# A graph network on one core: two chains of work put between the pieces of the second convolution, in a written order

## The chip, the cores and the metric

The kernel runs on one core of a Trainium2 chip. The metric is the device time of one execution in microseconds, the median of several. A profile is one execution, recorded instruction by instruction; its span runs from the first instruction to the last. Engines: PE multiplies (PEld loads its weights), DVE does vector work, ACT activations, POOL (GpSimd) indirect loads, memsets and iotas; SP issues most DMAs.

## The reference, cut to what matters

Four layers work on a graph of 6250 nodes with 64 features and 206250 edges, sorted by destination, each self loop included; each layer adds its result to x after a layer norm and a ReLU.

```
h = relu(layernorm(x))
x = x + conv(relu(conv(h, W3, b3)), W4, b4)        # conv: D^-1/2 (A + I) D^-1/2 h W^T + b
x = x + segment_sum(norm * h[col], row)            # h = relu(layernorm(x)), over src
V = leaky(leaky(h) @ pAw + pAb) @ pBw + pBb        # h again from x
e = relu(relu(edge_attr @ w1 + b1) @ w2 + b2)
M = clip(sigmoid(e @ Bw + Bb) * V[src] + e @ Cw + Cb, 1e-5) ** 2
x = x + sqrt(segment_sum(M, dst) / count)
out = x + mean of h and three propagations of it   # h = relu(layernorm(x))
```

## The kernel before, in words

Nodes are padded to 49 blocks of 128; seven blocks make a chunk (CB = 7, W = 896 nodes, NC = 7). A is the matrix of edge counts, in fp8, kept in DRAM in seven chunks of columns A[c]; a piece (A[c], block rows k) is 128 x 6272 bytes, 784 KB. Node values are held as three bf16 parts (U3 and V3, written by `split`, L707), so a sum over three products stands for float32.

The stages, in order:

1. **Building A and the first convolution** (`fast`, L752 to L993). Fourteen strips of 448 columns are built on PE, ACT and DVE and written to DRAM by SP. Beside the build of one strip, `convolve` (L934) multiplies the strip before by U3 into p_sum. When a chunk's two strips are done, `hidden` (L947) turns its sums y to nodes (L739), adds the node's own value, normalises, turns it to features (L731), applies W3 with a ReLU (L960, L961) and W4 (L965), and splits the result into V3. `convolve` and `hidden` are generators; each `yield` is a place where the builder puts other work. The last chunk's `hidden(6)` has nothing after it: L991 runs it to its end behind the last `convolve`.
2. **The second convolution** (`gather`, L1001, first call L1047). For chunk c and row k, one piece is loaded (pool `apool`, 8 buffers) and multiplied by V3: 49 products of 128 x 192 into four banks p_acc (L1016), opened by a product of zeros (L1013). After the seventh piece DVE sums the three parts (L1024), and `convolved` (L1037) adds b4 and the residual, normalises, and splits into a new U3. The pools of this call are closed behind it.
3. **The gather over src** (second call of `gather`, from L1054), in pools opened anew. `turned` (L1056) does after each chunk the residual, the norm, the two node layers on PE (L1065, L1070, L1076, with ACT L1068 and L1072), adds pBb (L1079, L1081) and writes the chunk to Vp_dram by SP (L1082). Vp_dram is complete when the seventh is written.
4. **The messages' preparations** (L1096 to L1160): w1, w2, b1, b2, BC and the bias are loaded by ACT's queue, BC_b, src_g and dst_g (the edges' ends, `[128, 202, 8]` int32) by SP's; the bias is split in three (L1116 to L1120); `rel`, `off`, `missed` (L1139 to L1145) count edges that lie outside their window; `lane` (L1148, L1150) is dst modulo 128; `origin` (L1136) and `count` (L1157) are made by POOL.
5. **The messages** (L1161 to L1418): 202 groups of 1024 edges. A slot issues eight indirect loads (`fetched`, L1273 on: L1279 on POOL, from Vp_dram by src_g) into a pool of four v tiles, the edge layers (L1287 to L1305), the gate, the sum by destination, and the check that A is symmetric (`crossed`, `partial`). The order on PE, ACT and DVE is written out by hand there.
6. **Three propagations** (from L1420), the first from sums made beside the messages, two by `gather`.

Outside the hand-written stretch, a scheduler places each engine's instructions by its own estimate of when their inputs are ready; each engine and each DMA queue then works its list in order. A tile that takes up the memory of a closed pool waits for the last use of what lay there. [...]

Of the kernel before, what the change touches and what calls it, by code (L numbers as in the profile page):

```python
# [616 lines left out]
def fast(ctx, tc, bad, x, src, dst, edge_attr, W3, b3, W4, b4, w1, b1, w2, b2, Bw, Bb, Cw, Cb,  # L617
# [132 lines left out]

    X = node.tile([P, NB, D], F32, name="X")
    nc.scalar.dma_start(X, x.rearrange("(b p) f -> p b f", p=P))  # L752
    early = ExitStack()
    early_pool = early.enter_context(tc.tile_pool(name="early_pool", bufs=1, reuse_waits="tile"))
    with ExitStack() as ph:
# [52 lines left out]

        rpool = ph.enter_context(tc.tile_pool(name="rpool", bufs=3, reuse_waits="tile"))
        opool = ph.enter_context(tc.tile_pool(name="opool", bufs=2, reuse_waits="tile"))  # L810
        spool = ph.enter_context(tc.tile_pool(name="spool", bufs=3, reuse_waits="tile"))
        wpool = ph.enter_context(tc.tile_pool(name="wpool", bufs=1, reuse_waits="tile"))

        key = ipool.tile([P, 2, GC * P], BF16, name="key")
# [11 lines left out]
        with ExitStack() as ps:  # L826
# [109 lines left out]
            def convolve(s, strip):  # L936

                p = psum.tile([P, 512], F32, name="p_sum", bufs=2)
                for q in range(NQ):
                    for b in range(q * NB // NQ, (q + 1) * NB // NQ):  # L940
                        spread(p, U3, b, strip[:, b, :], CW)
                    yield
                if s % 2 == 0:
                    y[s // 2] = wpool.tile([P, W], F32, name="y")
                nc.scalar.activation(y[s // 2][:, s % 2 * CW:(s % 2 + 1) * CW], p[:, :CW], AF.Copy)

            def hidden(c):  # L947

                z = wpool.tile([P, CB, D], F32, name="z", bufs=2)
                nc.scalar.activation(z, to_nodes(psum, y[c], CB), AF.Copy)  # L950
                yield
                add_whole(z, U3, c)
                nc.vector.tensor_mul(z, z, over_features(norm0[:, blocks(c)]))
                yield
                zT = to_features(wpool, psum, z)
                yield
                h = wpool.tile([P, W], F32, name="h")
                for lo_, hi_ in ((0, 512), (512, W)):
                    p_h = psum.tile([P, 512], F32, name="p_node")
                    nc.tensor.matmul(p_h[:, :hi_ - lo_], W3T, zT[:, lo_:hi_], start=True, stop=True)  # L960
                    nc.scalar.activation(h[:, lo_:hi_], p_h[:, :hi_ - lo_], AF.Relu, bias=b3_c)  # L961
                    yield
                p_v = psum.tile([P, 512], F32, name="p_node").rearrange("p (b f) -> p b f", f=D)
                for k in range(CB):
                    nc.tensor.matmul(p_v[:, k, :], h[:, k * P:(k + 1) * P], W4T,  # L965
                                     start=True, stop=True)
                yield
                u = wpool.tile([P, CB, D], F32, name="z", bufs=2)
                nc.vector.tensor_mul(u, p_v[:, :CB, :], over_features(norm0[:, blocks(c)]))
                split(u, V3, c)  # L970

            beside = []
            for s in range(CS):
# [13 lines left out]
                nc.sync.dma_start(strip_of(s, slice(0, NB)), strip)  # L987
                beside = [convolve(s, strip)]
                if s and s % 2 == 0:
                    beside.append(hidden(s // 2 - 1))  # L990
            for steps in beside + [hidden(NC - 1)]:  # L991
                for _ in steps:
                    pass  # L993

# [3 lines left out]
        nc.vector.tensor_mul(u, h, over_features(scale[:, blocks(c)]))  # L998
        split(u, U3, c)

    def gather(apool, wpool, psum, U3, then):  # L1001


        zeros = wpool.tile([P, 6 * D], BF16, name="zeros", bufs=1)
# [1 line left out]
        for c in range(NC):  # L1006
            p = [psum.tile([P, 512], F32, name=f"p_acc{q}") for q in range(4)]
            for k in range(NC):
                t = apool.tile([P, CB, W], COUNT, name="piece")
                nc.sync.dma_start(t, A[c][:, blocks(k), :])  # L1010
                for d in range(CB):
# [3 lines left out]
                    for b in range(CB):  # L1015
                        nc.tensor.matmul(  # L1016
                            p[d // 2][:, d % 2 * 3 * D:(d % 2 + 1) * 3 * D],
                            t[:, b, d * P:(d + 1) * P],
                            U3[:, k * CB + b, :, :].rearrange("p t f -> p (t f)"),
                            start=False, stop=(k == NC - 1 and b == CB - 1 and d in (1, 3, 5, 6)))  # L1020
            z = wpool.tile([P, CB, D], F32, name="zg")
            for q in range(4):
                n = min(2, CB - 2 * q)
# [3 lines left out]
                    axis=AX.X, op=OP.add)  # L1027
            then(c, z)

    with ExitStack() as ph:
        wpool = ph.enter_context(tc.tile_pool(name="wpool", bufs=2, reuse_waits="tile"))
        U3 = of_nodes(node)
        with tc.tile_pool(name="apool", bufs=8, reuse_waits="tile") as apool, \
                tc.tile_pool(name="ps1", bufs=1, space=PSUM, reuse_waits="tile") as psum:

            def convolved(c, z):
# [2 lines left out]
                nc.vector.tensor_add(z, z, over_blocks(b4_r, CB))  # L1041
                nc.vector.tensor_add(X[:, blocks(c), :], X[:, blocks(c), :], z)
                h = wpool.tile([P, CB, D], F32, name="h")
                normed_and_split(h, U3, c, norm3)

            gather(apool, wpool, psum, V3, convolved)

        pAw_d = diagonal(pAw, "pAw_d", wpool)
        pBw_d = diagonal(pBw, "pBw_d", wpool)
# [43 lines left out]
    Y = part.tile([P, CS, CW], F32, name="Y")  # L1093
    piece_pool = ctx.enter_context(tc.tile_pool(name="piece_pool", bufs=3, reuse_waits="tile"))
    with ExitStack() as ph:
        cpool = ph.enter_context(tc.tile_pool(name="cpool", bufs=1, reuse_waits="tile"))  # L1096
        before = ExitStack()
        tpool = before.enter_context(tc.tile_pool(name="tpool", bufs=1, reuse_waits="tile"))
        w1_d = diagonal(w1, "w1_d")
        w2_d = diagonal(w2, "w2_d")  # L1100
        b1_c = column(b1, 2, "b1_c")
        b2_c = column(b2, 2, "b2_c")

        BC = cpool.tile([P, 4 * D], F32, name="BC")
        nc.vector.memset(BC, 0.0)
        for k in range(2):
            nc.scalar.dma_start(BC[k * D:(k + 1) * D, 2 * k * D:(2 * k + 1) * D], Bw)
            nc.scalar.dma_start(BC[k * D:(k + 1) * D, (2 * k + 1) * D:(2 * k + 2) * D], Cw)

        bias = tpool.tile([1, 4, 2, D], F32, name="bias")  # L1110
        for k in range(4):
            nc.scalar.dma_start(bias[:, k, 0, :], Bb.unsqueeze(0))
            nc.scalar.dma_start(bias[:, k, 1, :], Cb.unsqueeze(0))
        rest = tpool.tile([1, 4, 2, D], F32, name="rest")
        bias3 = [tpool.tile([1, 4, 2, D], BF16, name=f"bias{k}") for k in range(3)]
        nc.vector.tensor_copy(bias3[0], bias)  # L1116
        nc.vector.tensor_sub(rest, bias, bias3[0])
        nc.vector.tensor_copy(bias3[1], rest)
        nc.vector.tensor_sub(rest, rest, bias3[1])
        nc.vector.tensor_copy(bias3[2], rest)  # L1120
        BC_b = cpool.tile([3, 8 * D], BF16, name="BC_b")
        for k in range(3):
            nc.sync.dma_start(BC_b[k:k + 1, :], bias3[k].rearrange("o a b f -> o (a b f)"))
        ones = cpool.tile([3, P], BF16, name="ones")
        nc.vector.memset(ones, 1.0)

        src_g = cpool.tile([P, G, J], I32, name="src_g")
        nc.sync.dma_start(src_g, src.rearrange("(g p j) -> p g j", p=P, j=J))
        dst_g = tpool.tile([P, G, J], I32, name="dst_g")
        nc.sync.dma_start(dst_g, dst.rearrange("(g p j) -> p g j", p=P, j=J))  # L1130

        origin = tpool.tile([P, G], F32, name="origin")
        g0 = 0
        for g in range(1, G + 1):
            if g == G or window(g) != window(g0):
                nc.gpsimd.memset(origin[:, g0:g], float(window(g0) * QN))  # L1136
                g0 = g
        rel = tpool.tile([P, G, J], F32, name="rel")
        nc.vector.tensor_tensor(rel, dst_g, origin.unsqueeze(2).to_broadcast([P, G, J]),  # L1139
                                op=OP.subtract)  # L1140
        off = tpool.tile([P, G, J], F32, name="off")
        nc.vector.tensor_scalar(off, rel, float(P), None, op0=OP.is_ge)
        nc.vector.tensor_scalar(rel, rel, 0.0, None, op0=OP.is_lt)
        nc.vector.tensor_add(off, off, rel)
        nc.vector.tensor_reduce(missed[:, 1:2], off.rearrange("p g j -> p (g j)"), axis=AX.X,  # L1145
                                op=OP.add)

        nc.vector.tensor_scalar(dst_g, dst_g, P - 1, None, op0=OP.bitwise_and)  # L1148
        lane = cpool.tile([P, G, J], BF16, name="lane")
        nc.vector.tensor_copy(lane, dst_g)  # L1150
        own = cpool.tile([P, P // QN, 2], F32, name="own")
        nc.vector.memset(own[:, :, 0], 0.0)
        for q in range(P // QN):
            nc.vector.memset(own[q * QN:(q + 1) * QN, :q + 1, 0], 1.0)
        nc.vector.tensor_scalar(own[:, :, 1], own[:, :, 0], -1.0, 1.0, op0=OP.mult, op1=OP.add)
        count = cpool.tile([P, P, J], BF16, name="count")
        nc.gpsimd.iota(count, pattern=[[1, P], [0, J]], base=0, channel_multiplier=0,  # L1157
                       allow_small_or_imprecise_dtypes=True)

        before.close()  # L1160
        mpool = ph.enter_context(tc.tile_pool(name="mpool", bufs=3, reuse_waits="tile"))  # L1161
        ps_a = ph.enter_context(tc.tile_pool(name="ps_a", bufs=1, space=PSUM, reuse_waits="tile"))
        n1 = stat.tile([P, NB], F32, name="n1")
# [252 lines left out]
        nc.vector.tensor_add(of_all[:, 0:1], of_all[:, 0:1], of_all[:, 2:3])  # L1416
        nc.vector.tensor_copy(bad, of_all[0:1, 0:1])


    with ExitStack() as ph:  # L1420
        apool = ph.enter_context(tc.tile_pool(name="apool", bufs=6, reuse_waits="tile"))
# [85 lines left out]
```

## Time and profile before

| what | value |
|---|---|
| time, median of 3 runs | 4138.98 us (4115.52 to 4143.48) |
| the profiled execution: its time, its span | 3623.47 us, 3621.6 us |
| mean granted TensorE clock | 0.909 |
| busy: PE, DVE, ACT, POOL | 84%, 54%, 34%, 46% of the span |
| chain that ended last | POOL 35%, PE 34%, issue 15%, DMA 8%, DVE 7% |
| 570 to 586 us | PE 10.92, DVE 1.32, ACT 3.43 us busy, PEclk 0.71 |
| 586 to 790 us (second convolution) | PE 204.00, DVE 69.81, ACT 9.87, POOL 0.00 us busy |
| 1019 to 1057 us | PE 8.71, DVE 16.62, ACT 1.58, POOL 0.00 us busy, PEclk 0.61 |
| 1057 to 3137 us (messages) | PE 1672.00, DVE 1195.59, ACT 851.40, POOL 1586.87 us busy |

How to read it: the chain of work is followed back from the last instruction, at each step to what released it; a row of it is start, duration and what ran. A row of the timeline is start, duration, engine, line, operation, tiles, count, and in brackets how long the engine had been idle and what ended that. PEclk is the clock that the throttle granted to TensorE, as a share of full speed. The profile is of one execution; its time and the timed runs' differ by 515 us.

### The profile page before, as it was taken

The page shows a single profiled execution, that of the slowest core. Times are in us where ns is not written, and L with a number is a line of the kernel's source. Part 1 is how long each engine was busy: PE and PEld are TensorE (multiplying, and loading weights), DVE is VectorE, ACT ScalarE, POOL GpSimd, SP SyncE. Part 2 cuts the span into 40 slices and gives each one's busy share as a digit, 9 for nine tenths or more (in the row PEclk, how much of TensorE's full clock was granted, in tenths as well). Part 3 has the DMA queues.
Part 4 walks back from the last instruction along what each step waited for, and adds up shares of the span by engine and source line. Part 5 has one row for each costly group of instructions (what it writes and reads, how often), then busy time and mean ns, then how long its engine had stood idle before and what let it go on. Part 6 is the DMA issues. An engine that isn't in the chain of part 4 may idle for free.

```text
span 3621.6 us, 59158 instructions
## 1 busy us (share of the span) xinstructions
PE 3035.6 (84%) x24193; PEld 2135.5 (59%) x24193; DVE 1948.4 (54%) x3904; ACT 1243.4 (34%) x2031; POOL 1650.3 (46%) x1870
## 2 busy tenths in 40 slices
PE   1699999999967777778888788877888878799999
PEld 0466667999944444444444444444444444489999
DVE  6899993332235546555555655655655565531111
ACT  1577771000014334334444443433434443210000
POOL 4200000000027777777777777777777777400000
PEclk9999999999978888888889888888888888899999
DMA  3233335655582322323333333322332322256664
GB/s 107 62 91 95 95 95 193 197 180 178 174 103 70 86 54 66 88 70 94 78 80 89 78 78 81 92 70 70 97 88 70 93 70 76 80 162 196 196 207 143
DMA packets 280496, 388.75 MB, mean 107 GB/s; under 512 B 189226, under 2 KB 191332, under 8 KB 279956
## 3 DMA queue, kind: packets, MB, share of 16 engines
q1 hardware_dynamic: 222260, 323.17, 29.7%
q0 software_dynamic: 54112, 58.92, 8.6%
q8 instruction: 192, 3.15, 0.4%
q10 hardware_dynamic: 3840, 2.77, 0.3%
q14 instruction: 92, 0.75, 0.1%
HBM read 340.47 MB, written 44.24 MB: 106 GB/s over the span
## 4 chain that ended last, share of the span: by engine, by line
POOL 35%; PE 34%; issue 15%; DMA 8%; DVE 7%; ACT 1%; POOLq 0%; DVEq 0%; ACTq 0%
POOL v L1279 35%; PE p_acc L1016 21%; PE p_sum L748 6%; DMA v<-Vp_dram,src_g 5%; PE p_a L857 3%; DVE hd L848 1%; DVE lo L848 1%; PE p_node L739 1%; DMA near<-pairs,begin_i 1%; PE p_bc L1305 1%; DMA src_g<-in_src 0%; PE p_node L960 0%; DMA run<-pairs,exact_i 0%; PE p_acc L1013 0%; PE p_node L965 0%
## 5 line engine op out<-in xcount | busy, mean ns | idle before, releaser
L1279 POOL DMA_INDIRECT v<-Vp_dram,src_g x1616 | 1586.9, 982 | 541.0 <-issue 462.9
L1016 PE MATMUL p_acc<-U,piece 128*128 128x192 bf16 x9604 | 816.6, 247 | 3.9 <-DMA piece<-A 3.9
L1016 PEld LDWEIGHTS <-piece 128*128 128x128 fp8e4 x9604 | 799.2, 98 | 15.6 <-DMA piece<-A 4.4
L1305 PE MATMUL p_bc<-BC,h 128*128 128x256 f32 x1616 | 579.0, 491 | 0.0
L1314 DVE TENSOR_TENSOR m<-gate,v 128x512 f32<-128x512 f32 x202 | 140.0, 693 | 763.7 <-DMA v<-Vp_dram,src_g 332.4
L1305 PEld LDWEIGHTS p_bc<-BC,h 128*128 128x128 f32 x1616 | 338.7, 232 | 152.5 <-issue 114.6
L1321 ACT ACTIVATE m<-m 128x512 bf16<-128x512 f32 x202 | 127.2, 630 | 817.2 <-DVE m L1316 817.2
L1136 POOL MEMSET origin<- 128x1 f32 (+1 forms) x194 | 6.5, 97 | 859.1 <-DMA piece<-A 859.1
L1024 DVE TENSOR_REDUCE zg<-p_acc 128x128 f32<-128x384 f32 x112 | 56.8, 508 | 598.7 <-PE p_acc L1016 598.2
L748 PEld LDWEIGHTS <-U 128*64 128x64 bf16 x4116 | 230.3, 113 | 217.4 <-issue 72.1
L861 ACT ACTIVATE strip<-p_a 128x784 fp8e4<-128x784 f32 x392 | 301.8, 820 | 104.0 <-PE p_a L857 103.0
L1301 PE MATMUL p_bc<-BC_b,ones 3*128 3x512 bf16 x404 | 179.2, 443 | 159.9 <-DVE m L1315 159.9
L1188 PE MATMUL p_sum<-ident_b,piece 128*128 128x128 bf16 x1372 | 154.1, 237 | 180.2 <-DVE junk L1194 179.9
L1188 PEld LDWEIGHTS <-piece 128*128 128x128 fp8e4 x1372 | 117.0, 106 | 314.8 <-issue 297.3
L1301 PEld LDWEIGHTS <-ones 3*128 3x128 bf16 x404 | 37.4, 93 | 431.4 <-DVE m L1315 231.2
L1291 PE MATMUL p<-h,w_d 128*128 128x512 f32 x404 | 255.7, 719 | 40.8 <-ACT h L1295 40.8
L748 PE MATMUL p_sum<-piece,U 128*64 128x448 fp8e4 x2058 | 238.4, 374 | 28.9 <-DVE junk L1194 20.7
L1295 ACT ACTIVATE h<-p,b_c 128x512 f32<-128x512 f32 x404 | 255.9, 684 | 13.5 <-PE p L1291 13.5
L1194 DVE SCALAR_TENSOR_TENSOR junk<-p_sum,there 128x512 bf16<-128x512 f32 (+1 forms) x392 | 242.4, 618 | 19.6 <-DMA there<-A 6.0
L748 PE MATMUL p_sum<-strip,U 128*64 128x448 fp8e4 x2058 | 236.8, 359 | 2.9 <-ACT U L711 1.4
L848 DVE TENSOR_TENSOR lo<-count,key 128x2048 bf16<-128x2048 bf16 x196 | 238.3, 1216 | 0.0
L857 PEld LDWEIGHTS <-lo 128*128 128x128 bf16 x3136 | 164.9, 103 | 102.7 <-DVE lo L848 80.3
(186 smaller groups left out, 3478.1 us busy)
## 6 DMA issues: line engine op xcount, KB each, us to landing
piece<-A SPq DMA_DIRECT2D x249, 784.0 KB
e<-in_edge_attr SPq DMA_DIRECT2D x202, 256.0 KB
A<-strip SPq DMA_DIRECT2D x14, 2744.0 KB
v<-Vp_dram,src_g POOLq DMA_INDIRECT x1616
there<-A SPq DMA_DIRECT2D x28, 784.0 KB
pairs<-pair SPq DMA_DIRECT2D x1, 1616.0 KB
Vp_dram<-v SPq DMA_DIRECT2D x7, 224.0 KB
out<-X SPq DMA_DIRECT2D x6, 224.0 KB
```

The lines of the kernel that those rows point to most:

```text
L748: nc.tensor.matmul(p[half * D:(half + 1) * D, :w], U3[:, b, k, :], at_block, start=(i < 2), stop=(i >= 3 * n - 2))
L848: nc.vector.tensor_tensor(t, of.unsqueeze(1).to_broadcast(t.shape), key[:, k, at:at + GB].rearrange("p (h j) -> p h j", j=GQ) .unsqueeze(2 ...
L857: nc.tensor.matmul(p[:, j, :2 * NB], lo[:, g // GQ, :, g % GQ], hd[:, g // GQ, :, g % GQ], start=True, stop=True)
L861: nc.scalar.activation(strips[s][:, :, col:col + 2 * SG].rearrange("p b (j l) -> p b j l", l=2), p[:, :, :2 * NB].rearrange("p j (b l) -> ...
L1016: nc.tensor.matmul(p[d // 2][:, d % 2 * 3 * D:(d % 2 + 1) * 3 * D], t[:, b, d * P:(d + 1) * P], U3[:, k * CB + b, :, :].rearrange("p t f - ...
L1188: nc.tensor.matmul(p[:, a - a0, :], held["here"][:, a, b * P:(b + 1) * P], ident_b, start=True, stop=True)
L1194: nc.vector.scalar_tensor_tensor(junk[:, :(a1 - a0) * P], p[:, :a1 - a0, :].rearrange("p a q -> p (a q)"), 15.5, there, op0=OP.min, op1=OP ...
L1279: nc.gpsimd.indirect_dma_start(out=v[:, j, :], out_offset=None, in_=Vp_dram[:, :], in_offset=bass.IndirectOffsetOnAxis(ap=src_g[:, g, j:j ...
L1291: nc.tensor.matmul(of[g][p], w, of[g].pop(x), start=True, stop=True)
L1295: nc.scalar.activation(of[g][t], of[g].pop(p), **how)
L1301: nc.tensor.matmul(p_bc[:, 4 * b:4 * b + 4].rearrange("p j o f -> p (j o f)"), ones, BC_b, start=True, stop=False)
L1305: nc.tensor.matmul(p_bc[:, 2 * q:2 * q + 2].rearrange("p j o f -> p (j o f)"), h2[:, q * P:(q + 1) * P], BC, start=False, stop=(k == 1))
```

## The change

- `hidden(NC - 1)` is no longer run behind the first convolution. It is given the second convolution's pools and its steps are issued between that one's pieces.
- The preparations of stage 4 become a generator, `prepared`, whose steps follow those of `hidden` in the same places. Its results lie in a pool at the other end of the memory (`side="right"`), where the strips' pool is moved too, and stay until the messages end.
- `gather` takes the steps (`beside`): two after each of the first five pieces of chunk 0, then one after each piece. The first call runs under a hand-written order for PE and DVE.
- BC, the bias and BC_b are loaded by GpSimd. src and dst are no longer loaded in runs of eight ints: four loads by GpSimd bring rows of 1024 ints (`rows_i`, 101 partitions), DVE turns them to float32, PE transposes them 4 x 101 columns at a time into a bank p_turn (two banks), and DVE copies them into src_g and dst_g.
- The second convolution's `apool` has 7 buffers for 8. The new U3 is made at the first chunk's end. The y of the last two strips lies in the pool that V3 lies in.

```diff
-        spool = ph.enter_context(tc.tile_pool(name="spool", bufs=3, reuse_waits="tile"))
+        spool = ph.enter_context(tc.tile_pool(name="spool", bufs=3, side="right", reuse_waits="tile"))
...
-                    y[s // 2] = wpool.tile([P, W], F32, name="y")
+                    y[s // 2] = (wpool if s < CS - 2 else early_pool).tile([P, W], F32, name="y")
...
-            for steps in beside + [hidden(NC - 1)]:
+            for steps in beside:
...
-    def gather(apool, wpool, psum, U3, then):
+    def gather(apool, wpool, psum, U3, then, beside=iter(())):
...
+                for _ in range(2 - (c > 0 or k > 4)):
+                    next(beside, None)
...
+    def prepared(psum):
+
+        cpool = apart.enter_context(tc.tile_pool(name="cpool", bufs=1, side="right", reuse_waits="tile"))
...
+            nc.gpsimd.dma_start(BC[k * D:(k + 1) * D, 2 * k * D:(2 * k + 1) * D], Bw)
...
+        def row(i):
+            rows_i.append(tpool.tile([GH, P, J], I32, name="rows_i", bufs=2))
+            nc.gpsimd.dma_start(rows_i[i], halves_of[i][0])
+
+        row(0)
+        row(1)
+        for _ in range(6):
+            yield
+        for i in range(4):
+            rows_f = tpool.tile([GH, J, P], F32, name="rows_f", bufs=2)
+            nc.vector.tensor_copy(rows_f, rows_i[i].rearrange("g p j -> g j p"))
+            if i < 2:
+                row(i + 2)
+            yield
+            for j0 in range(0, J, 4):
+                p = psum.tile([P, 4, GH], F32, name="p_turn", bufs=2)
+                for j in range(4):
+                    nc.tensor.transpose(p[:, j, :], rows_f[:, j0 + j, :], ident[:GH, :GH])
+                nc.vector.tensor_copy(halves_of[i][1][:, :, j0:j0 + 4],
+                                      p.rearrange("p j g -> p g j"))
+                yield
...
-        with tc.tile_pool(name="apool", bufs=8, reuse_waits="tile") as apool, \
+        with tc.tile_pool(name="apool", bufs=7, reuse_waits="tile") as apool, \
...
-            gather(apool, wpool, psum, V3, convolved)
+            with tc.manual_schedule(engines={ET.PE, ET.DVE}):
+                gather(apool, wpool, psum, V3, convolved, (
+                    step for steps in (hidden(NC - 1, wpool, psum), prepared(psum))
+                    for step in steps))
...
-        src_g = cpool.tile([P, G, J], I32, name="src_g")
-        nc.sync.dma_start(src_g, src.rearrange("(g p j) -> p g j", p=P, j=J))
-        dst_g = tpool.tile([P, G, J], I32, name="dst_g")
-        nc.sync.dma_start(dst_g, dst.rearrange("(g p j) -> p g j", p=P, j=J))
...
+        cpool, w1_d, w2_d, b1_c, b2_c, BC, BC_b, ones, src_g, lane, own, count = made.pop()
```

The lines left out of `prepared` are those of stage 4, cut in steps by `yield`: the bias and BC_b, then `rel`, then `off` and `missed`, then `lane`, `own` and `count`.

## The prediction

> **What bounds the kernel now.** I read the slices of the page first (PE at 0.9 in the first third, then POOL at 0.7 while PE stays at 0.7 to 0.8), then the chain that ended last, then the timeline around the change. The chain gives PE 34% and POOL 35% (all L1279) of the span: first PE bound, then, from 1057 to 3137 us, bound by GpSimd's 1616 fetches. Two places in between are bound by neither. The chain in order of time, at the end of the first convolution:
>
> ```profile
> 556.74 14.16 PE p_sum L748 x147
> 570.90 1.75 PE p_node L739 x14
> 577.48 2.08 PE p_node L960 x2
> 580.33 1.66 PE p_node L960 x2
> 582.64 3.25 PE p_node L965 x14
> 586.21 2.24 PE p_acc L1016 x14
> 588.77 1.93 PE p_acc L1016 x14
> 592.18 24.83 PE p_acc L1016 x301
> ...
> 790.73 4.57 DMA piece<-A
> ```
>
> Between 570.90 and the first p_acc work at 585.68 stands one chain through PE, ACT and DVE (`hidden(6)`), with nothing beside it. The p_acc groups of 14 after it take 2.24 us and 1.93 us, where 301 take 24.83 us (82.5 ns each, so 14 take 1.16). At 790.73 the gather by src waits 4.57 us for its first piece.
>
> The same view, from the end of that gather to the first fetch:
>
> ```profile
> 1000.64 17.83 PE p_acc L1016 x216
> 1018.48 0.02 issue
> 1018.49 17.71 DMA src_g<-in_src
> ...
> 1037.19 5.25 DMA bias<-in_L_gnn_Cb
> ...
> 1043.00 7.77 DMA BC_b<-bias
> 1050.77 1.83 DVE rel L1139
> ```
>
> 38.6 us pass between the last matmul on this chain and the first fetch, and they go to loading and preparing, in series. The timeline shows who waits for whom:
>
> ```profile
> 1036.80 0.30 ACT L701 ACTIVATE v<-v,eps 128x7 f32<-128x7 f32 x1 [38.09 <-DMA bias<-in_L_gnn_Bb]
> 1053.23 0.39 SPq L1082 DMA_DIRECT2D Vp_dram<-v  x1
> 1057.11 2.33 POOL L1279 DMA_INDIRECT v<-Vp_dram,src_g  x1 [48.75 <-DVE lane L1150]
> ```
>
> The last chunk's own work (its ACT square root) is held at 1036.80 behind the bias loads on ACT's queue, its addition of pBb behind `rel` on DVE, and the fetch waits for `lane`.
>
> **What the Trainium skill says.** "TensorE: Matmul & The Clock Gate", section "What's actually happening": an idle window of some 3.4 us halves the array's clock, and about as much work restores it. The trace agrees: PEclk is 0.79 at 576 to 577, 0.50 from 577 to 590, 0.88 in the next us. "DMA: Bandwidth & Descriptors", section "Why small descriptors are slow": each packet carries a fixed cost. The trace agrees: src_g, 808 KB in runs of 8 ints (32 B), took 17.71 us while the DMA share stood at 1.4 to 2.0 and 54 to 69 GB/s moved, where pieces move at 400 to 450 GB/s (568 to 584 us). Section "Issuing engines are not separate DMA queues": loads from GpSimd share the 16 engines, so the row loads will run among the pieces; no run shows that yet.
>
> **The change part by part**, against the profiled span of 3621.6 us. A minus is time gained.
>
> *Start.* The built order shows W3's and W4's loads now behind five square roots on ACT's queue, and the copy to W3T ahead of the 25 L802 counts on DVE. The fifth root ran at 32.48. The load then takes 2.65 us (as the small `near` gathers do) to 4.5 us (10.58 to 15.04 before), with PE 0.76 us: ready at 36.0 to 37.8, where DVE got there at 36.0. I take +1.0 (0 to +2.5).
>
> *hidden(6) into the gather.* Before: p_acc would have had to start at 587.92 to be, at full pace, where it was at 590.54 (two groups of 1.31 us back), so the stretch costs 587.92 - 570.90 = 17.0. After: pieces flow from 568.5 at about 0.4 MB/us, so the first lands near 571 and PE waits about 1.3. hidden's PE work at full clock is 1.71 (14 by 122 ns) + 0.60 + 0.45 + 1.12 (as L1070 in the gather) + 0.84 + 1.71 = 6.4. Its steps are issued in pairs, so PE still sits through the feature copies (1.0 and 0.57) and the last ReLU (0.67): 2.2; 0.6 for changing over. 17.0 - 10.5 = **-6.5** (-4 to -8.5). The other waits (y, z) pass under a piece of 4.1 us. V3's last block is ready after piece 3 and read at piece 6.
>
> *Pieces' pool, 8 to 7.* The 49 pieces end in slot 6, not 0. In the built program the next gather's first five pieces wait for matmuls of the last chunk's pieces 0 to 4, not for its last one. Before: 790.71 to 795.35 idle, then 112 matmuls in 10.90 us (9.24 at full pace): 6.3. After: the four zero matmuls wait for the last sum, ended at 791.09: 0.8. **-5.5** (-4 to -6). Seven buffers are still 28 us ahead.
>
> *Preparations into the gather, on PE.* 32 transposes of 101 columns; four of 128 took 0.66 (L1065), so 8 x 0.52 = 4.2. DVE is in written order: chunk 0's chain ends 10.9 us after chunk 1's first matmul (627.76 - 616.85), the first row cast comes behind it, and its transposes behind piece 1, at 8.75. The cast of 1024 ints in strides takes 0.63 (by L1150's 0.99 for 1616) to 1.17 (by L1139's 1.84); I take 1.1: PE waits 12.0 - 8.7 = 3.3. Later transposes find their cast done and their bank read (17 against 12). **+7.6** (+4.5, no stall, to +15, one us for each group).
>
> *The same on DVE, ACT, POOL.* About 21 us of DVE (four casts, eight copies of some 0.55, bias 2.6, the L1139 to L1150 group 9.5) lie in a stage where DVE worked 70 of 204 us; chunk ends stay clear: chunk 2's `rel` ends near 28, its first sum is wanted at 27 and PE needs it by 30. Were that cover gone, `rel`'s 1.8 would be added. POOL is idle there; its memsets and iota stand ahead of the waits. Behind the later row loads only BC_b waits on POOL. ACT's four diagonal loads wait for early pieces and stand before chunk 0's square root, 15 us ahead of need. The rows (404 KB each) cost, by the page's 2.0 + bytes/436e3 us ("Anatomy of one DMA"), an estimated 2.9 us. The third row is asked for at 12 and wanted near 31, so 0.
>
> *After the gather.* Gone from the path: src_g, dst_g, eight bias loads, BC_b, rel and lane. What remains is the chunk's chain. In chunk 5 it went from L1057 at 990.01 to the write's issue at 1001.40: 11.4. The last one runs at half clock (1.09, 2.08, 2.04 against 0.66, 1.12, 1.16): +2.3. From 1022.93 it issues at 1036.6. Then the write must land: at most 3.6 (1053.23 to 1056.84); by the page's formula about 2.5. I take 3.0 and 0.3: fetch at 1039.9. 1057.1 - 1039.9 = **-17.2** (-15.5 to -18.5).
>
> Does the earlier start reach the end? POOL's fetches idle 541 us, 462.9 of it their own issue, 48.8 this start, 25.6 buffers. So it is passed on in full. The first e load follows the write at once; PE starts on it some 5 us after the fetch, as before.
>
> Sum: 1.0 - 6.5 - 5.5 + 7.6 - 17.2 = -20.6: span 3601. The profiled execution took 3623.5, the timed runs 4139 (4115.5 to 4143.5); no view shows the 515 us between, so I subtract the same time: **4118**.
>
> **Rivals.**
> - *The earlier fetches are not passed on*: the messages end with something else, and the first three parts alone are left (-3.4): 4136. For it: PE is busy 80% there. Against: the chain stays on L1279. 0.09.
> - *Timed runs stretch the removed waits*: they are 14% longer than the profile. If the removed loads and waits are what is stretched, about double, the gain is 41: 4097 or less. Against: 14% as such makes 23.5. 0.12.
> - *Row loads late*: DVE stands at the third cast (chunk 1, piece 6), the chunk's sums are queued behind it, PE waits for them. Each us beyond 31 adds one. Slower than before from 19 of margin + 20.6 of gain, a load of 40 us; at 60 it gives 4139 + 20 = 4159. For it: 14 pieces queue on the same engines. Against: src_g, twice the bytes in small packets, took 17.7. 0.06.
> - *The moves do not happen* is excluded: the built order shows them on PE, DVE, POOL and SP.
>
> **How the numbers follow.** The forecast has 0.73, its own range 4103 to 4133 (the parts' ends, and the three runs' scatter of 28). About 1%, 41 us, is what a measurement of this kernel can tell from no change. Faster by more: 0.13 (the second rival and an edge of scatter). Slower by more: 0.04, of the third. Within: 0.83. The range that leaves out 2 in 10 is 4092 to 4143.
>
> **What would show it.** p_acc starts near 572 with groups of 14 near 1.2 us from the start; p_node and p_turn between pieces; one PE wait for the first cast of about 3 us; no wait for a piece at the next gather; the fetch some 17 us after the last sum, released by the Vp_dram write. Wrong if PE waits for rows or DVE at chunk ends, if the gather of the first stage grows by over 25 us, or if the fetches' stretch (2080 us) grows.

## The result, and the profile after

| | before | after |
|---|---|---|
| median of 20 runs | 4141.14 us | 4125.14 us |
| lowest to highest | 4115.52 to 4176.94 | 4093.77 to 4160.34 |
| ratio, 95% interval | | 0.9954 (0.9935 to 0.9973) |

The ratio is 19 us in 4141 (11 to 27); it leaves out the runs that count as slow, over 1.5% above the fastest of their kernel, while the two medians, 16 us apart, are those of all 20 runs. The forecast was 4118 us, the kernel before less 20.6. The profiled execution of the kernel after has a span of 4132.5 us and a clock of 0.847.

The times of one and the same kernel come in two sets, by the group of runs. In one the medians of the kernel before are 4141 to 4171 us, and single runs lie up to some 40 us to either side; in the other it takes 3619 to 3627 us. Each group of the experiments ran on one chip, so the text speaks of chips of the first kind (the long times) and of the second; that it is the chip, and not something else about the group, is not shown. The first profile of the kernel before (3621.6 us) is of the second kind, the profile of the kernel after is of the first. So stages are compared here from the moment when SP issues the last strip's write, and the kernel before was profiled again on a chip of the first kind (`before_again`, below). Those two profiles give, in us after the strip's write ("in between" is the change since the row above):

| | before_again | after | difference | forecast |
|---|---|---|---|---|
| strip's write issued (from the start) | 562.29 | 562.66 | +0.4 | +1.0 |
| chunk 1 of the second convolution starts | 59.96 | 56.73 | -3.2 | -6.5 |
| last chunk ended, next gather opens | 233.64 | 238.86 | +8.5 in between | +7.6 |
| chunk 1 of the src gather starts | 267.85 | 267.93 | -5.1 in between | -5.5 |
| last sum on DVE ended | 465.60 | 465.66 | 0.0 in between | 0 |
| first fetch | 499.84 | 482.70 | -17.2 in between | -17.2 |

The first fetch comes 17.1 us sooner. Where that comes from can be read in the views of the kernel after. Its chain of waits at the end of the first convolution:

```profile
563.28 17.35 DMA piece<-A
580.67 1.37 PE p_acc L1017 x14
582.36 2.24 PE p_acc L1017 x14
584.92 1.38 PE p_acc L1017 x14
586.46 0.58 PE p_acc L1017 x7
587.03 1.54 PE p_node L739 x14
588.57 4.04 PE p_acc L1017 x49
...
603.38 15.61 PE p_acc L1017 x189
```

`hidden(6)` now stands between pieces (p_node after seven products of p_acc), as the change says. But the first piece lands 17.35 us after its issue. p_sum is done at 576.9 (ACT copies y at 576.88), so PE waits 3.8 us for the piece, where 1.3 was forecast, and the second group of 14 takes 2.24 us, where 1.16 is the full pace: half clock again.

The preparations take time from PE in chunk 1 (first the timeline, then the chain):

```profile
630.94 1.07 DVE L1073 CAST rows_f<-rows_i 101x1024 f32<-101x1024 int32 x1
632.07 0.56 PE L1080 MATMUL p_turn<-ident,rows_f 101*128 101x101 f32 x4 [3.78 <-DVE rows_f L1073]
```

```profile
632.63 5.70 PE p_acc L1017 x49
638.33 0.35 PE p_turn L1080 x4
638.68 8.09 PE p_acc L1017 x98
```

PE waits once, 3.78 us, for the first cast. Then a piece of 49 products takes 5.70 us, where two pieces take 8.09 (4.04 each). After the first one, a group of four transposes takes 0.35 us; 0.52 was forecast.

At the next gather there is no wait for a piece, only the one for the last sum:

```profile
801.69 0.77 PE p_acc L1014 x4
802.46 27.56 PE p_acc L1017 x334
```

And the end of the src gather, in the chain and in the timeline:

```profile
1033.83 1.10 PE p_node L1175 x4
1035.02 0.61 ACT hT L1178
1035.66 2.09 PE p_a L1180 x2
1037.78 0.70 ACT aT L1182
1038.49 0.70 DVE aT L1183
1039.33 2.06 PE p_v L1186 x8
1042.13 2.20 DMA Vp_dram<-v
```

```profile
1045.36 1.03 POOL L1325 DMA_INDIRECT v<-Vp_dram,src_g  x1 [363.51 <-issue]
```

src_g, the bias, `rel` and `lane` are gone from this stretch. What is left is the last chunk's own work on PE, about twice as long as in the other chunks (2.09 and 2.06 us where p_a and p_v take 1.14 and 1.16), and its write.

### The profile page after: what moved, and what is told of

It is laid out like the page before. It is cut to its first block, busy times and chain, and to the rows that moved or that the text cites. A ratio compares the mean times of both kernels' runs of the same rounds, so it can differ in the third digit from the quotient of the medians.

```text
span 4132.5 us, 59248 instructions
## 1 busy us (share of the span) xinstructions
PE 3161.0 (76%) x24225; PEld 2164.1 (52%) x24225; DVE 1984.4 (48%) x3916; ACT 1257.3 (30%) x2031; POOL 1663.9 (40%) x1889
## 4 chain that ended last, share of the span: by engine, by line
PE 51%; DVE 16%; another core or an unknown queue 13%; issue 9%; ACT 7%; DMA 2%; POOL 1%; DVEq 0%; SPq 0%; ACTq 0%; POOLq 0%
PE p_acc L1017 18%; PE p_sum L748 9%; PE p_bc L1351 7%; PE p L1337 5%; PE p_a L858 3%; DVE junk L1240 2%; ACT h L1341 2%; PE p_s L1379 2%; DVE m L1361 2%; DVE m L1360 2%; PE p_bc L1347 2%; PE p_e L1333 2%; DVE m L1362 1%; ACT gate L1356 1%
## 5 line engine op out<-in xcount | busy, mean ns | idle before, releaser
L748 PE MATMUL p_sum<-piece,U 128*64 128x448 fp8e4 x2058 | 272.4, 384 | 80.9 <-issue 59.6
L1337 PE MATMUL p<-h,w_d 128*128 128x512 f32 x404 | 270.0, 752 | 73.6 <-ACT h L1341 58.8
L1424 ACT ACTIVATE m<-m 128x512 bf16<-128x512 f32 x202 | 127.3, 630 | 594.0 <-DVE m L1423 468.6
L1379 PE MATMUL p_s<-m,to 128*128 128x192 bf16 x1616 | 207.0, 276 | 117.9 <-DVE r_s L1387 61.7
L1337 PE MATMUL p<-eT,w_d 128*128 128x512 f32 x404 | 250.2, 705 | 17.7 <-issue 8.1
L1367 ACT ACTIVATE m<-m 128x512 bf16<-128x512 f32 x202 | 127.2, 630 | 431.0 <-DVE m L1362 342.8
L1379 PEld LDWEIGHTS <-to 128*128 128x128 bf16 x1616 | 174.1, 150 | 145.3 <-issue 141.3
```

The source lines that it names most:

```text
L748: nc.tensor.matmul(p[half * D:(half + 1) * D, :w], U3[:, b, k, :], at_block, start=(i < 2), stop=(i >= 3 * n - 2))
L1337: nc.tensor.matmul(of[g][p], w, of[g].pop(x), start=True, stop=True)
L1379: nc.tensor.matmul(p, to[:, :, j], m3[:, j].rearrange("p t f -> p (t f)"), start=(j == 0), stop=(j == J - 1))
```

## The experiments

**The kernel before again (`before_again`, no edit).**

> The kernel before, unchanged, profiled again beside the others. Question: where do the 515 us lie that the timed runs of before take over its first profile (3621.6), and do the stretches that the change removes get longer with them? Theory (the forecast's): they lie elsewhere, in the messages above all (the kernel after spends some 2500 us there, against 2080 in the first profile of before), and from the last sum of the src gather to the first fetch it stays near 38.6 us, from the first convolution's strip to the end of chunk 0 near 60.3 us. Rival (removed waits are stretched): those two stretches are some 14% to 100% longer, 44 to 77 us and 69 us up, and the change should have brought more than it did. Span expected near 4137 by both.

The span is 4169.4 us. From the last sum to the first fetch it takes 34.2 us, as in the first profile (466.19 to 500.39 after the strip's write), and from the strip's write to chunk 1 it takes 59.96 us against 60.13. So the stretches that the change removes are not longer on this kind of chip, and the rival of stretched waits falls. (The expectation's 38.6 counts from PE's last product, not from the sum.) The time lies in the fetches: from the first to the last it is 2604.7 us against 2078.1, 526.6 more. Another 5.6 lie before the strip's write, and 16 behind the last fetch. In the fetches the chain that ended last is another one. Its shares by engine over the whole of before_again:

```profile
PE 53%; DVE 16%; another core or an unknown queue 12%; issue 9%; ACT 7%; DMA 2%; POOL 1%; DVEq 0%; SPq 0%; POOLq 0%; ACTq 0%
```

In the first profile POOL had 35% of it; here it has 1%. GpSimd waits 550.6 us, in 106 waits, for DVE (L1314) to give back a v tile, and DVE, ACT and PE in turn stand still for stretches whose releaser no view names.

**One part alone: `hidden(6)` (`hid_only`).** From the kernel before: the strips' pool, the y of the last two strips and the new U3 as in the kernel after, and

```
-            gather(apool, wpool, psum, V3, convolved)
+            with tc.manual_schedule(engines={ET.PE, ET.DVE}):
+                gather(apool, wpool, psum, V3, convolved, hidden(NC - 1, wpool, psum))
```

> One part alone: only hidden(6) goes between the pieces; the preparations stay behind the src gather and are loaded as before, and the pieces' pool keeps its eight buffers. In the profile of the kernel after, the stretch from the strip's write to the end of chunk 0 shrank by 3.9 us, not by the forecast 6.5: the first piece came 17.4 us after its issue and PE idled 3.8 us for it. Theory A: the eight bias loads and the two row loads that GpSimd issues at the same moment took engine time ahead of that piece. Then here, without them, the first p_acc comes some 15 us after the strip's write is issued, PE idles under 2 us, no clock is lost, and the stretch is 53.5 to 55 us against 60.3 (gain 5.5 to 7). Theory B: the piece would have come no sooner anyway; then p_acc comes 18 us after and the gain is 3.9 again. The median: 4 to 7 us below the kernel before (ratio 0.998 to 0.999), within what the rounds can tell.

The first product into p_acc comes 15.5 us after the strip's write (the piece is issued at 564.34 and takes 14.83), so PE waits the forecast 1.3 us. Every group of 14 takes 1.16 to 1.33 us, and chunk 1 starts at 52.55, 7.4 us sooner than before. Theory A holds: without GpSimd's loads the part is worth its forecast, and a little more. With eight buffers the next gather's chunk 0 takes 34.34 us. The first fetch comes at 494.39, only 5.4 sooner: here SP's queue has src_g behind the last Vp_dram write, and the fetch waits for that load (17.12 us). The ratio is 0.9955 (0.9924 to 0.9986). The interval just leaves out what 5.4 us would give (0.9987), and no view explains why the timed runs gain more than the earlier fetch.

**The other part alone: the preparations (`prep_only`).** From the kernel after:

```
-            for steps in beside:
+            for steps in beside + [hidden(NC - 1, wpool, psum)]:
...
-                gather(apool, wpool, psum, V3, convolved, (
-                    step for steps in (hidden(NC - 1, wpool, psum), prepared(psum))
-                    for step in steps))
+                gather(apool, wpool, psum, V3, convolved, prepared(psum))
```

> The other part alone: hidden(6) runs to its end behind the first convolution as before, only the preparations go between the pieces (two steps after each of the first five), with seven buffers. Theory: fetch 17 us after the last sum (38.6 before, so about -21 with the cold chain's start counted alike), no wait for a piece at the next gather (-5.5), PE longer by 8 transposes groups and one wait for the first cast. The steps come eight earlier than in the kernel after, so the first cast stands in chunk 0, before any chunk's chain holds DVE: PE's wait for it should be about 1 us or none, not 3.8, and the gather of this stage +3 to +4 us rather than +8.4. Sum -19 to -22: ratio 0.9945 to 0.9955, so nearly all of the gain of the whole change. Rival (the earlier fetches are not passed on): ratio 0.999 to 1.0.

The end of the src gather is as expected (17.0 us from the last sum to the first fetch), and that gather's chunk 0 takes 29.07. PE's part is not as expected. There is no wait for a cast in chunk 0, but the third row's cast falls behind chunk 0's chain on DVE, and PE waits for it 4.34 us in chunk 1, which takes 36.57. That is the same wait at another cast. The first fetch comes at 486.29, 13.5 us sooner. The ratio is 0.9981 (0.9956 to 1.0007), that is 8 us less, with an interval from 18 less to 3 more: it holds the 13.5 and does not tell it from nothing.

**Is an earlier fetch passed on? (`late_fetch`)** The kernel after, with

```
+                if c == NC - 1:
+                    for _ in range(64):
+                        nc.vector.tensor_scalar(v, v, 1.0, None, op0=OP.mult)
```

> The kernel after, with 64 multiplications by one of the last chunk's v on DVE ahead of its write to Vp_dram (a chain of 64 x 0.5 to 0.65 us): the first fetch comes some 32 to 42 us later, and nothing else is changed. Theory (a later start of the fetches reaches the end in full): the time is 32 to 42 us above the kernel after, so about 15 to 24 us above the kernel before (ratio to before 1.003 to 1.006). Rival (not passed on: the messages end with something else, and in the timed runs GpSimd waits some 500 us for buffers): the time stays that of the kernel after, ratio 0.9955; a half passed on would give 1.000.

The multiplications follow each other every 0.43 us, so the fetch comes 28.5 us later than in the kernel after (511.2 after the strip's write). The ratio is 1.0037 (1.0016 to 1.0059), which is 0.0083 above the kernel after: 34 us (22 to 46, from the two intervals). A delay passed on in full lies inside this, a half (14 us) does not. So on this kind of chip too, where GpSimd waits for buffers, a later start of the messages moves their end. The edit holds DVE itself as well as the fetches, so it does not tell which of the two does it.

**First cast two pieces later (`shift`): `range(6)` becomes `range(8)`. Loads later (`later_rows`):**

```
         bias = tpool.tile([1, 4, 2, D], F32, name="bias")
+        nc.vector.memset(bias, 0.0)
...
+            if i < 2:
+                nc.vector.memset(rows_i[i][:, :1, :], 0)
             nc.gpsimd.dma_start(rows_i[i], halves_of[i][0])
```

> The kernel after with all steps from the first row cast on two pieces later (eight empty steps instead of six). In the kernel after, chunk 1 of the second convolution took 36.00 us instead of 28.95: PE waited 3.78 us for the first cast, which stands behind chunk 0's chain on DVE, and ran the next 49 products in 5.70 us instead of 4.04. Theory: the first transposes then come behind the fourth piece of chunk 1, 16.2 us after its start, when the cast (ended 12.6 us after the start) is done; no wait, no lost clock, so chunk 1 about 29.5 to 30.5 us, chunk 2 about 30.4, chunk 3 about 29.6, and what all groups of transposes cost together is eight times 0.35 = 2.8 us instead of 8.5. Rival: the wait moves with the step (DVE is late for another reason, or the rows themselves come late): then some chunk still takes 33 us or more.

> The kernel after, with a small memset on DVE ahead of the eight bias loads and of the first two row loads, so that GpSimd issues them some 40 us later (as it does BC's), not at the moment when the first pieces are fetched. Theory A (these loads delay the first piece): with only hidden moved, the first p_acc came 15.5 us after the strip's write was issued and chunk 0 ended at 52.6; with the loads there it came at 18.0 and chunk 0 ended at 56.7. Here 15.5 and 52.5 to 53.5 again, and the first cast in chunk 1 no later than before (rows there by 615 us). Theory B (something else of the preparations delays chunk 0): 56 to 57 again.

These and the next two ran on a chip of the second kind (median of before: 3621.24). The chain of shift, where the loads start with the first pieces, and that of later_rows:

```profile
557.77 17.40 DMA piece<-A
575.21 2.42 PE p_acc L1017 x14
```

```profile
558.18 14.82 DMA piece<-A
573.05 1.33 PE p_acc L1017 x14
574.38 0.16 PE p_acc L1014
574.54 1.16 PE p_acc L1017 x14
```

Theory A holds for later_rows: the piece is back at 14.8 us and chunk 1 starts at 52.54, against 57.69 in shift and 56.73 in the kernel after. Up to there these kernels differ in nothing but the start of ten loads by GpSimd, and three small memsets. The traces show what the loads delay. In the five profiled kernels that start them there (the kernel after twice, late_fetch, shift, after_right), on chips of both kinds, the packets of the two row loads run from about 9.6 to 14.5 us after the issue of the strip's write, and that write, which SP issued ahead of the first piece, ends 15.5 to 15.7 us after its issue. In all others, before included, it ends at 13.0 to 13.1. So the piece's 2.5 us are lost while the strip's write still runs ahead of it.

For shift neither theory holds. Chunks 1 and 2 take 31.29 and 32.76 us. The 3.8 us wait is gone, but the later steps now stand at the ends of chunks. There a cast or a copy is ahead of the sums on DVE, and PE waits 1.14 us for its banks at the end of chunk 1 and of chunk 2, and 0.55 us for the third cast, which stands behind chunk 1's chain. All preparations together cost PE 6.2 us, where they cost 8.5.

**The edits of shift and later_rows in one kernel (`both`).**

> Both repairs in one kernel: the row and bias loads later, the first cast two pieces later. Theory: the first fetch, 482.7 us after the strip's write in the kernel after and 499.8 in the kernel before, comes at 482.7 - 4.2 - 5.7 = 473 us, 27 us sooner than before, and this reaches the end in full: ratio to before 0.9935 (after: 0.9954; the two intervals may overlap). Rival: a gain so small in the gather is taken back by a wait at a chunk's end (DVE's steps now lie in chunk 3): fetch at 476 us or later.

The first fetch comes at 476.4, the rival's number, for the reason just seen. The ratio is 0.9966 (0.9955 to 0.9977), 12 us (8 to 16). But the first fetch comes 24 us sooner than in the first profile of before, which is of the same kind. So part of the lead is lost on the way: 7 us of it between the profiled executions (3621.6 to 3605.0 us), half of it in the timed runs.

**No transposes: the small runs back, but in the gather (`direct`).** Everything from `GH = G // 2` to the last transpose is replaced (and the bias memset kept):

```
+        for t, ends in ((src_g, src), (dst_g, dst)):
+            nc.vector.memset(t[:, :, :1], 0)
+            nc.scalar.dma_start(t, ends.rearrange("(g p j) -> p g j", p=P, j=J))
+        for _ in range(18):
+            yield
```

> The same places, but no casts, transposes and copies: src_g and dst_g are loaded in runs of eight ints as in the kernel before, by ACT's queue, while the pieces of chunk 0 and 1 are read; the bias later as in the run beside it. Theory A (the loads in small runs are hidden where PE is the bound): PE does nothing for them (0 of 2.8 us), the pieces' loads are seven buffers ahead and lose at most 2 x 17.7 us of engine time beside a share that stood at 0.51 to 0.60: fetch at about 470 us after the strip's write, ratio 0.993. Theory B (the small packets crowd out the pieces): PE waits for pieces in chunk 1 or 2 by 10 to 25 us, fetch at 480 to 495, ratio 0.996 to 1.0; then rows and transposes are the better way.

Theory A holds. Chunks 1 to 6 take 28.95 us each; PE never waits for a piece there, though the two loads keep the DMA engines busy. The first fetch comes at 470.11, 30.3 us sooner. The ratio is 0.9932 (0.9918 to 0.9945), 25 us (20 to 30), so some 5 us are lost on the way here too. Where? At the last fetch, in the chains of before (first profile), direct, and direct_right2 (below), all on a chip of the second kind:

```profile
3135.24 3.22 DMA v<-Vp_dram,src_g
```

```profile
3102.80 8.02 DMA v<-Vp_dram,src_g
```

```profile
3105.88 2.94 DMA v<-Vp_dram,src_g
```

and what SP issues then, in the timelines of the same three:

```profile
3138.59 2.00 SPq L1456 DMA_DIRECT2D piece<-A  x4
```

```profile
3095.46 46.40 SPq L1483 DMA_DIRECT2D piece<-A  x7
```

```profile
3119.53 19.88 SPq L1483 DMA_DIRECT2D piece<-A  x7
```

In the kernel before, the pieces of the first propagation start 3.4 us behind the last fetch. In direct they start 7.3 us ahead of it, and the last rows land among 784 KB pieces, 8.0 us after their issue. From the last fetch to the end it takes 491.4 us instead of 486.4 (491.0 and 491.4 in later_rows and shift, 492.6 in both). In the built program of before the first of these pieces takes the memory of the last group's v tile, so it waits for the last fetches to land. With the preparations' pool moved to the other end of the memory (the built program of after), it takes that of the group before the last, and waits for that one's loads and DVE's product. The trace of direct agrees: that product ends at 3095.43, and the piece is issued at 3095.46.

**Kernel after again (`after_again`), and the propagations' pool moved (`after_right`, `direct_right`):**

```
-        apool = ph.enter_context(tc.tile_pool(name="apool", bufs=6, reuse_waits="tile"))
+        apool = ph.enter_context(tc.tile_pool(name="apool", bufs=6, side="right", reuse_waits="tile"))
```

> The kernel after, unchanged, beside two others on one chip. Two sets of times have been seen for the kernel before: near 4140 to 4170 us, and on another chip (as in its first profile) 3619 to 3627 us with hardly any scatter. By stages the kernel after reaches its first fetch 17.1 us sooner than before after the strip's write (482.7 against 499.8). Where the fetches pace the messages (the second set), two edits built on it (both, direct) lost some 5 us of their lead between the last fetch and the end: the pieces of the first propagation are asked for 6 to 7 us before the last fetch instead of 3.4 us after it, and the last fetch took 8 us instead of 3.4 to reach DVE. Theory: the kernel after has the same loss, so it gains 17 - 5 = 12 us on such a chip (ratio 0.9967) and 17 to 19 us on one of the first kind (0.9955), where the last fetch is not what the end waits for. Rival: the lead of 17 us arrives in full on both.

> The kernel after with one word added: the propagations' pieces pool is opened at the other end of the memory (side right), over the preparations' tiles, so that its first piece waits for the last group's sum instead of for an earlier v tile. Theory: the pieces then start some 12 us after the last fetch, the last fetch reaches DVE after 3.4 us again, and the time is 5 us below that of the kernel after on a chip where the fetches pace the messages (no change on one of the other kind). Rival: the loss comes from something else at the end (a last group with more work in it), then nothing changes; or the second piece, which now waits for the last count (24 us after the last fetch), comes late and takes back 3 to 8 us.

> The direct loads (src_g and dst_g by ACT's queue in small runs, the bias later, nothing on PE) with the same word added. direct gave 0.9932 (0.9918 to 0.9945), 23.4 us, of a lead of 30.3 us at the first fetch. Theory: 5 us more, so about 28 us: ratio 0.992 where the fetches pace the messages. Rival: as before, 0.9932.

They ran on a chip of the first kind. after_again has 0.9959 (0.9934 to 0.9984), the first result once more. after_right has 0.9974 (0.9952 to 0.9996) and direct_right 0.9947 (0.9924 to 0.9969). The three intervals overlap and tell nothing of the pool's place. In all three, and in the kernel after, the last fetch is issued 22 to 31 us before DVE works on its group, so the end does not wait for it.

**Once more, on the second kind (`direct_right2`):**

> The direct loads with the propagations' pool at the other end of the memory, once more: the question about the last fetch can only be told on a chip where the fetches pace the messages (the kernel before at 3619 to 3627 us); the last such runs fell on one where they do not. If it is such a chip here: theory, the first propagation's pieces start 12 us after the last fetch, the last fetch reaches DVE 3.4 us after its issue (8.1 in direct), the end comes 486 us after the last fetch (491.4 in direct), ratio to before 0.9915 to 0.9925 (direct: 0.9932). Rival: 491 us and 0.9932 again. If it is the other kind: ratio 0.9947 again (0.9924 to 0.9969), and the question stays open.

The theory holds. The pieces start 13.6 us behind the last fetch, which lands in 2.94 us, and from there to the end it takes 486.0 us. The ratio is 0.9909 (0.9893 to 0.9926), 33 us (27 to 39); what was expected, 0.9915 to 0.9925, lies inside. The profiled executions differ by 29.7 us (3621.6 to 3591.9), which is the lead of 30 us at the first fetch, passed on whole. The intervals of direct and direct_right2 overlap slightly, so the times alone would not tell them apart; the profiles do.

## Why the prediction was right

By stages the two profiles differ by 16.6 us where 20.6 were forecast (+0.4 - 3.2 + 8.5 - 5.1 - 17.2). The interval of the timed runs (11 to 27) holds both numbers; that their 19 comes closer to the forecast than its own terms do is luck.

- *Start.* +0.4 for +1.0: W3T's copy ends at 35.98, where DVE had come by then, so there is no wait. The strip's write lies 0.1 to 0.9 us later than in the first profile in shift, later_rows, both and direct too.
- *hidden(6) into the gather.* -3.2 for -6.5, outside its own range. The failed term is "PE waits about 1.3": it was 3.8, and the half clock behind it cost the rest. The step took the first piece's landing from a profile in which GpSimd loaded nothing at 557 to 571 us, and gave GpSimd's rows and bias no cost at that moment. They start at 562.95, beside the strip's write and ahead of the pieces. hid_only and later_rows show it, by -7.4 without them and 4 to 5 us regained. The estimate of 2.9 us for a row load does not hold there either: the first two, issued at 567.19 and 569.52, are in at 577.1. The other two, issued at 632.3 and 640.6, take 3.0 and 3.3 us. The Trainium skill's "DMA: Bandwidth & Descriptors", section "Issuing engines are not separate DMA queues", which the forecast had named, says just this: loads of all queues interleave on the same engines. It was named and then not applied to that moment. The trace agrees: 14.8 us for the first piece without them, 17.35 with them.
- *Pieces' pool.* -5.1 for -5.5; 34.21 to 29.07 us for the chunk. It goes with the number of buffers in every run (34.34 in hid_only with eight, 29.07 in prep_only with seven); no run changed that number alone.
- *Preparations on PE.* +8.5 for +7.6, made of other terms, whose errors partly cancel: 8 x 0.35 = 2.8 for 4.2 (the price was scaled from transposes with other shapes), 3.8 of wait for 3.3, and 1.7 of lost clock behind it that the sum left out. The Trainium skill's "TensorE: Matmul & The Clock Gate", section "What's actually happening", says that an idle window of some 3.4 us halves the clock. The trace agrees: the 3.78 us wait is followed by 49 products in 5.70 us instead of 4.04. A wait forecast at 3.3 stood so close to it that the loss should have been named in the range's upper end.
- *After the gather.* -17.2, as forecast, and by its terms: 13.8 us from the last sum to the write's issue (11.4 + 2.3 forecast), 3.2 from there to the fetch (3.3), of which the write took 2.20 to land.
- *Passed on in full.* The number is right for the first kind of chip (late_fetch; 17 us of lead, 19 of time, 11 to 27), but not by the prediction's reason, which was that POOL paces the fetches: POOL has 35% of the chain in the first profile of before and 1% in that of the kernel after. That an earlier start is passed on there is shown; why, is open. The sign "the fetches' stretch grows" has to be read on one kind of chip as well: 2574.7 us in the kernel after, 2604.7 in before_again, so it has not grown. On the second kind four edits lost about 5 us at the last fetch. The kernel after itself ran on no such chip; that it loses the same is argued from the edits that share its pools.
- *The 515 us.* "No view shows" them, and taking them over unchanged was right: before_again places them behind the first fetch.
- *Rivals.* Stretched waits: fallen (before_again). Not passed on: fallen (late_fetch). Late rows: DVE did not wait for any row here (the third was asked for at 632.3 and cast at 652.0). A load slow enough to hold it was not tried.

## What to carry to other kernels

A load that is wanted late is not free: it costs where it starts. Give it something to wait for; otherwise it may delay a transfer that is urgent, as here. A step on DVE in a written order costs PE by its place: behind a chunk's chain PE waits for the step, ahead of the chunk's sums PE waits for the sums. And where a pool is moved to another end of the memory, the pools opened later may take other memory too: look which tile each first transfer of the later stages then waits for.

## What was not expected of the hardware

- Two loads of 25,856 runs of 32 bytes each kept the engine that issued them: ACT stood 28.90 us at the second one's issue ("599.86 28.90 ACTq L1060" in direct's timeline), and its next square root came behind it, at 628.80. The packets of the two, 1.7 MB, ran from 601 to 649 us, beside 7.1 MB of pieces, and PE lost nothing. In 600 to 660 us ACT's queue took 65.7% of the DMA engines' time.
- The same kernel has a median of 3621 us on one chip and of 4171 on another, at mean granted clocks of 0.91 and 0.85. In before_again 46 stretches of over 3 us, 239 us in sum, have PE, DVE and ACT idle together during the fetches; in the first profile there is one, of 4.8 us. DMA packets take about the same mean time in both (90 and 87 ns for GpSimd's queue during the fetches, 143 and 142 ns for SP's). What stops the engines there is open.
